# Eighty-seven gathered rows fetched by SyncE in a deformable-convolution kernel

## The chip, the cores and the metric

The kernel runs on one core of one Trainium2 chip. The metric is the device time of the whole launch in microseconds (us). The engines of the core are TensorE (PE; its weight loads are listed apart as PEld), VectorE (DVE), ScalarE (ACT), GpSimd (POOL) and SyncE (SP). SP does no arithmetic here: it issues DMAs through its own queue (SPq). POOL issues the indirect DMAs (gathers).

## The reference, cut to what matters

The input is x, 4 images of 128 channels and 128 x 128 pixels. Two layers are computed; all that matters for this change lies in the first step of layer 0, a deformable 3 x 3 convolution on the channel-normalised image:

```python
offset = conv(x, w_off)                       # 18 offsets for each pixel
py, px = base_y + dy, base_x + dx             # 9 sampling points (taps) for each pixel
sampled = sum over 4 corners of x[:, corner] * bilinear weight
out = einsum('bckhw,ock->bohw', sampled, w_conv)
```

Where a pixel samples depends on the data, so its four corners must be fetched by an index that is known only at run time. After it come a mixture of 8 experts (top 2), a Fourier-domain channel mix, which the kernel does as a flip and one matmul, and a router over 64 experts that picks 8 tokens for each; their results are added to those tokens.

## The kernel before, in words

**Tables.** For each image the kernel normalises the channels and writes a table to HBM (`table_of`, line 688, and `block`, line 530). An entry of the table is 1 KB: two image rows of one column, 128 channels each. Two neighbouring entries, 2 KB in one piece, hold the four corners of a sampling point. `positions` turns the offsets into the index of the first entry (line 677) and into four weights. The offsets themselves come from a convolution by matmuls over padded rows: `padding` (line 458) copies four transposed rows into one of four pad tiles, and `offsets` (line 467) runs six matmuls over two of them. Image 0's table is built at the start; the table of each next image is built while the present one is sampled.

**Sampling.** An image has 32 groups of four rows, a group has 9 taps, and one tap of one group is a `Chunk` (line 764): 288 an image, 1152 in all. For a chunk, `gather` (line 771) has POOL issue four indirect DMAs, one for each row, each fetching 128 positions x 2 KB into the tile `g` (128 x 4 x 4 x 128 float32). `weighted` has DVE multiply three of the rows by their weights (all four where the tap is 0); `weighted_too` has ACT do the fourth row in four instructions; `summed` has PE transpose and add the corners (16 transposing matmuls into PSUM, named trg); `moved` has ACT copy that to sT; and eight matmuls or more add it to `sums` by the convolution's weights (`convolved`, line 734). The pool of `g` has AHEAD = 6 buffers, so the gathers of chunk n + 6 are issued when PE has read chunk n.

**Order.** Every engine works through its instructions in the order in which they are written out. The main loop (line 1621) writes chunk after chunk; each chunk is two turns (`tick`). `Turns` (line 117) runs the rest as small jobs that yield for some turns: the experts, the flip, the router, the next image's table. SP's instructions stand in that same order: a DMA of SP that waits for an engine holds up every later one of SP. In the sampling SP carries the table stores (table<-ent), the loads of the image (xc, xg) and the stores of finished rows (x_d<-x).

SP's DMAs take eight completion semaphores in turn. A DMA that takes one first waits until the DMA that had it before has landed, so at most eight of SP's DMAs are under way. POOL's gathers have eight semaphores of their own.

**What else the change touches.** A tile of zeros, `blank` (line 342), is the weight of the matmul that clears `sums`. While image 3 is sampled, expert weights are loaded into places that are free by then, among them the first 512 columns of the four pads (`flat_pads`, lines 335 and 1655).

Of the kernel before, what the change touches and what calls it, by code (L numbers as in the profile page):

```python
# [42 lines left out]
F32 = mybir.dt.float32  # L43
I32 = mybir.dt.int32
U32 = mybir.dt.uint32
AF = mybir.ActivationFunctionType
ALU = mybir.AluOpType
AX = mybir.AxisListType
# [3 lines left out]
P = 128  # L52
# [5 lines left out]
HID = 512  # L58
# [6 lines left out]
TAPS = 9  # L65
EPS_C = 1e-6
EPS_T = 1e-5
RB = 8
CB = 16
TW = P + 1  # L70
TC = P + 2
# [14 lines left out]
BANKS = 6  # L86
AFTER = 11
SPACE = 13
BLOCK = 84
FILL = "fill"  # L90
DONE = "done"
# [98 lines left out]
def metaformer_kernel(  # L190
# [50 lines left out]
    with ExitStack() as main:  # L241
# [91 lines left out]
        for pad in pads:  # L333
            nc.vector.memset(pad, 0.0)
        flat_pads = [pad.rearrange("p y x -> p (y x)")[:, 0:HID].unsqueeze(1) for pad in pads]
        aT_sb = wts.tile([P, P], F32, name="aT_sb")

        gwT_sb = wts.tile([P, 2 * E1], F32, name="gwT_sb")
        gb_sb = wts.tile([P, 1], F32, name="gb_sb")


        blank = wts.tile([P, P], F32, name="blank")
        nc.vector.memset(blank, 0.0)
        flip = wts.tile([P, P], F32, name="flip")
        nc.gpsimd.memset(flip, 0.0)
        for base in (0, -P):
# [108 lines left out]
                yield from with_bias(ew_sb[:, 4 * h : 4 * h + 4, :], biases[h])  # L455


        def padding(t, h, row, read, padded):

            yield FILL  # L460
            tr = transposes(row, 4)
            read.append(h)
            yield turns.hop
            eng.scalar.copy(pads[(2 * t + h) % 4][:, :, 1 : P + 1], tr)
            padded.append(h)

        def offsets(im, t, padded):

            while len(padded) < 2:
                yield 1  # L470
            yield 1


            yield FILL
            po = bank([P, 4, P], "po")
            for k in range(3):
                for h in range(2):
                    eng.tensor.matmul(
                        po[h * P // 2 : (h + 1) * P // 2],
                        lhsT=woff_sb[:, k, :],  # L480
                        rhs=pads[(2 * t + h) % 4][:, :, k : k + P],
                        start=(k == 0),
                        stop=(k == 2),
                    )
            yield turns.hop
# [13 lines left out]
            yield turns.hop  # L499
            if i0 == 0:  # L500
                im.z[q] = pa.tile([P, CB + 2, 6 * TAPS], F32, name=f"z{im.b}_{q}", tag="z")
                if q == 0:
                    eng.vector.memset(im.z[q][:, 0, :], 0.0)
                else:
                    eng.scalar.copy(im.z[q - 1][:, CB + 1, :], tr[:, 0, 0, 0 : 6 * TAPS])
            eng.scalar.copy(
                im.z[q][:, 1 + i0 : 1 + i0 + RB, :].rearrange("p (h i) o -> p h i o", h=2),
                tr[:, :, :, 0 : 6 * TAPS].rearrange("p i h o -> p h i o"),
            )
            if i0 == 0 and q > 0:  # L510
# [192 lines left out]
        class Group:  # L703
# [30 lines left out]
            def convolved(self, k):  # L734

                yield 1
                if k + 1 < FIRST:
                    return
                if k + 1 == FIRST:
                    eng.tensor.matmul(  # L740
                        sums.rearrange("p s c -> p (s c)"),
                        lhsT=blank,
                        rhs=iota,
                        start=True,
                        stop=False,
                    )
# [13 lines left out]
                if k + 1 == TAPS:  # L760
                    yield turns.hop
                    yield from mixed(self)

        class Chunk:


            def __init__(self, group, k):
                self.group, self.k = group, k
                self.shared = k > 0

            def gather(self):
                self.g = pg.tile([P, 4, 4, P], F32, name="g", tag="g")
                im = self.group.im
                for s, y in enumerate(self.group.rows):
                    eng.gpsimd.indirect_dma_start(
                        out=self.g[:, s].rearrange("p v c -> p (v c)"),
                        out_offset=None,
                        in_=im.table,
                        in_offset=bass.IndirectOffsetOnAxis(
                            ap=im.index[:, y, self.k : self.k + 1], axis=0  # L780
                        ),
                    )

            def weighted(self):
                n = 3 if self.shared else 4
# [4 lines left out]
                )  # L790

            def weighted_too(self):
                g, y = self.g[:, 3], self.group.rows[3]
                w = self.group.im.weight[y // CB]
                for v in range(4):
                    eng.scalar.activation(
                        g[:, v, :], g[:, v, :], AF.Copy, scale=w[:, y % CB, self.k, v : v + 1]
                    )

            def summed(self):  # L800

                self.tr = bank([P, 4, P], "trg")
                for s in range(4):
                    for v in range(4):
                        eng.tensor.matmul(
                            self.tr[:, s, :],
                            lhsT=self.g[:, s, v, :],
                            rhs=ident,
                            is_transpose=True,
                            start=(v == 0),  # L810
                            stop=(v == 3),
                        )

            def moved(self):
# [2 lines left out]
                eng.scalar.copy(group.sT[self.k], self.tr)  # L817
                turns.start(group.convolved(self.k))


        exps = []

# [766 lines left out]

        def in_turn():  # L1590

            for b in range(NB):
                for number, (rows_of, minus, runs) in enumerate(orders[b]):
                    im = images[b]
                    if im.sent <= P // RB or not im.weight.keys() >= {y // CB for y in rows_of}:
                        raise ValueError("a table is late")
                    group = Group(images[b], number, rows_of, minus, runs)
                    group.begin()
                    for k in range(TAPS):
                        chunk = Chunk(group, k)  # L1600
                        chunk.gather()
                        yield chunk

        source = in_turn()
        chunk = [next(source) for _ in range(AHEAD)]
        turns.hop = HOP
# [5 lines left out]
        def tick(more):  # L1612

            turns.fills(0)
            turns.slot += 1
            if more and total - QUICK <= n <= total:
                turns.steps()
                turns.fills(0)
                turns.slot += 1

        while n < total + 3 or turns.jobs:
# [14 lines left out]
            if 0 <= n < total:  # L1636
                chunk[n].summed()
                turns.fill()
            tick(False)
            if 0 <= n - 1 < total:  # L1640
                chunk[n - 1].moved()
            turns.steps()
            if n >= 0 and n + 3 < total and (n + 3) % TAPS == 0:
                chunk[n + 3].group.weights((n + 3) // TAPS % 2)
            tick(True)
            if n == LATE * slots:
# [8 lines left out]
                rooms = [[part(), part()], [part(), part()], flat_pads]  # L1655
# [100 lines left out]
```

## Time and profile before

| | |
|---|---|
| Time, median of 3 runs | 7746.31 us (7738.57 to 7773.56) |
| The profiled execution: its own time | 7753.58 us |
| Its span, first to last instruction | 7751.8 us |
| Sampling, first gather to the last trg | 120.1 to about 7569 us |
| Mean granted TensorE clock | 0.879 |
| DMA bytes moved | 1526.15 MB, 1210.35 of them on the gathers' queue |

All times are of one execution. Busy shares are means over the whole span. A group of the page's list is named by line, engine, operation and tiles; nearly all instructions are recorded by one helper, line 104, so the tiles tell what they are. "Idle before" is time in which the engine did nothing ahead of an instruction of the group, with what ended it: "issue" means that nothing the profile shows was waited for.

### The profile page before, as it was taken

The numbers are of one execution on the slowest core, as the hardware profiler recorded it, in microseconds if no ns is written. First come the engines' busy times: TensorE is split into PE (matmuls) and PEld (weight loads), VectorE is DVE, ScalarE is ACT, GpSimd is POOL, SyncE is SP. The second block draws the span as 40 slices with busy tenths as digits, with TensorE's granted clock in tenths as the row PEclk, the third lists the DMA queues.
The fourth block names the chain that finished last, engine by engine and source line by source line (L and its number), as shares of the span: only waits on it lengthen the run. The fifth ranks groups of instructions, "written<-read, shape, count | busy, mean of one in ns | idle before, by whom it ended". The sixth has DMA issues, their size and how long they took to land.

```text
span 7751.8 us, 118020 instructions
## 1 busy us (share of the span) xinstructions
PE 6164.8 (80%) x38823; PEld 4942.0 (64%) x38823; DVE 4872.4 (63%) x15420; ACT 3844.8 (50%) x9910; POOL 4474.6 (58%) x4795
## 2 busy tenths in 40 slices
PE   5778888788878878888788788888777888888875
PEld 3666666666666666666666666666666666767663
DVE  5566666666566666666666666666667655666663
ACT  4455555554455555554455555555444444454442
POOL 5655555556555555565655555555666656655650
PEclk8888888888888889898888898888888998898987
DMA  7566665666665666665666666666655676777657
GB/s 223 177 196 184 190 193 184 193 182 180 189 191 181 188 188 189 190 192 176 188 189 189 189 188 189 190 188 183 197 179 173 221 256 184 240 266 258 186 170 266
DMA packets 579234, 1526.15 MB, mean 197 GB/s; under 512 B 86456, under 2 KB 225408, under 8 KB 578624
## 3 DMA queue, kind: packets, MB, share of 16 engines
q0 software_dynamic: 369664, 1210.35, 51.3%
q1 hardware_dynamic: 206656, 299.87, 11.5%
q8 instruction: 310, 5.08, 0.3%
q10 hardware_dynamic: 2304, 8.39, 0.3%
q14 instruction: 300, 2.46, 0.1%
HBM read 1381.43 MB, written 136.85 MB: 196 GB/s over the span
## 4 chain that ended last, share of the span: by engine, by line
PE 66%; issue 17%; DVE 7%; ACT 3%; another core or an unknown queue 3%; DMA 3%; POOL 2%; POOLq 0%; DVEq 0%; ACTq 0%; SPq 0%
PE trg L104 27%; PE sums L104 16%; PE pe L104 11%; PE tr L104 4%; PE po L104 3%; DVE g L104 2%; DMA g<-table,index 2%; DVE x L104 2%; POOL g L104 2%; PE ps L104 1%; PE small L104 1%; PE pq L104 1%; PE pf L104 1%; ACT g L104 1%
## 5 line engine op out<-in xcount | busy, mean ns | idle before, releaser
L104 POOL DMA_INDIRECT g<-table,index x4608 | 4375.0, 949 | 3030.1 <-issue 1251.6
L104 PE MATMUL trg<-ident,g 128*128 128x128 f32 x18432 | 2705.5, 300 | 774.3 <-issue 691.1
L104 PEld LDWEIGHTS trg<-ident,g 128*128 128x128 f32 x18432 | 2400.3, 157 | 1058.2 <-issue 944.1
L104 DVE TENSOR_TENSOR g<-g,small 128x1536 f32<-128x1536 f32 (+1 forms) x1152 | 2075.3, 1805 | 769.4 <-remote 349.4
L104 DVE SCALAR_TENSOR_TENSOR x<-pe,gate,x 128x128 f32<-128x128 f32 x4072 | 1394.1, 343 | 930.2 <-PE pe L104 512.8
L104 PE MATMUL sums<-wconv_sb,sT 128*128 128x128 f32 x9216 | 1389.7, 291 | 452.8 <-issue 407.5
L104 PEld LDWEIGHTS sums<-wconv_sb,sT 128*128 128x128 f32 x9216 | 1251.0, 203 | 697.9 <-issue 657.3
L104 ACT COPY sT<-trg 128x512 f32<-128x512 f32 x1152 | 667.6, 580 | 2063.3 <-remote 906.4
L104 ACT ACTIVATE g<-g,weight 128x128 f32<-128x128 f32 x4096 | 1303.4, 393 | 26.3 <-DMA g<-table,index 22.9
L104 PE MATMUL pe<-ew_sb,nT 128*128 128x512 f32 x2048 | 1119.1, 649 | 31.3 <-issue 26.7
L104 PEld LDWEIGHTS pe<-ew_sb,nT 128*128 128x128 f32 x2048 | 372.3, 213 | 221.2 <-issue 191.8
L104 DVE TENSOR_TENSOR x<-ps,x 128x512 f32<-128x512 f32 x128 | 87.9, 687 | 414.2 <-remote 254.2
L104 ACT ACT_TABLE_LOAD x263 | 337.4, 1283 | 7.5 <-DVE nmax L104 2.2
L104 ACT ACTIVATE n<-x,b_nb,b_rs 128x128 f32<-128x128 f32 x512 | 210.2, 482 | 142.6 <-DVE b_nb L104 52.2
L104 ACT ACTIVATE xn<-x,c_nb,c_rs 128x128 f32<-128x128 f32 x512 | 211.3, 485 | 137.6 <-DVE c_nb L104 72.9
L104 DVE BATCH_NORM_STATS2 b_st<-x 128x6 f32<-128x128 f32 x512 | 136.3, 283 | 191.4 <-ACT x L104 93.8
L104 ACT ACTIVATE tn<-x,d_nb,d_rs 128x128 f32<-128x128 f32 x512 | 210.9, 483 | 57.0 <-DVE d_nb L104 48.5
L104 ACT ACTIVATE c_rs<-c_mv,eps_c 128x4 f32<-128x4 f32 x128 | 38.0, 297 | 401.5 <-DVE c_mv L104 266.7
L104 PE MATMUL po<-pad,woff_sb 128*64 128x512 f32 x768 | 199.6, 633 | 4.0 <-issue 3.7
L104 PEld LDWEIGHTS sums<-ident,xg 128*128 128x128 f32 x1024 | 139.7, 196 | 84.5 <-issue 84.3
L104 PE MATMUL small<-rw_sb,nT 128*128 128x8 f32 x1024 | 140.7, 252 | 64.8 <-issue 63.2
L104 PEld LDWEIGHTS small<-rw_sb,nT 128*128 128x128 f32 x1024 | 141.2, 206 | 59.5 <-issue 57.5
(236 smaller groups left out, 5326.2 us busy)
## 6 DMA issues: line engine op xcount, KB each, us to landing
g<-table,index POOLq DMA_INDIRECT x4608
table<-ent SPq DMA_DIRECT2D x48, 1024.0 KB
xc<-in_x SPq DMA_DIRECT2D x64, 512.0 KB
w<-x_d SPq DMA_DIRECT2D x64, 512.0 KB
xg<-in_x SPq DMA_DIRECT2D x124, 256.0 KB
x_d<-x SPq DMA_DIRECT2D x124, 256.0 KB
out<-w SPq DMA_DIRECT2D x48, 512.0 KB
w<-in_weight SPq DMA_DIRECT2D x42, 512.0 KB
```

What stands on the lines that cost most here:

```text
L104: return self.tc.keep_in_program_order(issue(*args, **kwargs))
```

## The change

87 of the 4608 row gathers are taken from POOL and given to SP. A class `Lone` chooses, once every 13 chunks (RUN), a coming chunk whose tap isn't 0 and whose table is complete. For that chunk POOL gathers three rows; the fourth, the one that ACT weights, is fetched by SP:

- DVE scales the row's 128 indices to byte offsets (one instruction on 128 x 1). SP stores them to HBM and, seven turns later, loads them back as 4 x 32 integers in four partitions.
- SP loads them into registers, sixteen at a time, and after each load issues sixteen DMAs of 2 KB, one for each position, each written as two pieces of 1 KB. There are five DMAs a turn, so a row takes 26 turns, and the next row follows at once.
- The rows land in two tiles in turn. They are the pads 2 and 3, which the tables' `padding` gives up while sampling goes on: it then has two pads instead of four, and a job that finds its pad taken waits (`busy`).
- The chunk that uses the row is weighted some six to seven turns after the row's last DMA is written out.
- `blank` becomes the first 128 columns of another tile of zeros, and two of the `flat_pads` places for expert weights become two tiles of the pool of weights.

```diff
+        apart = [
+            pad.rearrange("p y x -> p (y x)")[:, 0:HID].rearrange("p (v c) -> p v c", c=P)
+            for pad in pads[2:]
+        ]
+        busy = [False, False]
+        places = [wts.tile([4, P // 4], I32, name=f"places{i}") for i in range(2)]
+        scaled = [wts.tile([P, 1], I32, name=f"scaled{i}") for i in range(2)]
...
+        def pad_of(t, h):
+            return pads[(2 * t + h) % 4 if turns.hop == 1 else h]
...
+            while turns.hop > 1 and busy[h]:
+                yield 1
+            busy[h] = True
...
                 for s, y in enumerate(self.group.rows):
+                    if s == 3 and self.lone is not None:
+                        continue
                     eng.gpsimd.indirect_dma_start(
...
+            def look(self, t):
+
+                i, begin = len(self.users), max(t + 16, self.end)
+                n = (begin + 2 * RUN + 7) // 2 + 1
+                n += n % TAPS == 0
...
+            def job(self, i, n, im, index, begin):
+                row = self.found[i]
+                eng.vector.tensor_scalar(scaled[i % 2], index, 8.0 * P, None, ALU.mult)
+                yield
+                yield
+                eng.sync.dma_start(out=row.unsqueeze(1), in_=scaled[i % 2])
+                for _ in range(7):
+                    yield
+                eng.sync.dma_start(out=places[i % 2], in_=row.rearrange("(a c) -> a c", a=4))
+                while self.now < begin:
+                    yield
...
+                for p in range(P):
+                    if p % 16 == 0:
+                        a, c = divmod(p, P // 4)
+                        loads, values = nc.values_load_multi_w_load_instructions(
+                            places[i % 2][a : a + 1, c : c + 16],
+                            engines=[mybir.EngineType.SP],
...
+                    eng.sync.dma_start(
+                        out=apart[i % 2][p : p + 1]
+                        .rearrange("p (h v) c -> p h (v c)", h=2)
+                        .bitcast(U8),
+                        in_=flat[bass.ds(values[p % 16], 16 * P)]
+                        .rearrange("(o h c) -> o h c", o=1, h=2),
+                    )
+                    if p % (P // (2 * RUN) + 1) == P // (2 * RUN):
+                        yield
...
+            def turn(self, t):
+                self.now = t
+                if self.filling is not None and next(self.filling, DONE) is DONE:
+                    self.filling = None
+                if self.ahead is None:
+                    self.look(t)
+                if self.ahead is not None:
+                    next(self.ahead)
...
+                lone.turn(2 * n)
             tick(False)
...
+                lone.turn(2 * n + 1)
```

More of the change, by code (lines that the diff above doesn't have):

```diff
@@ L45 @@
 U32 = mybir.dt.uint32
+U8 = mybir.dt.uint8
 AF = mybir.ActivationFunctionType
@@ L88 @@
 SPACE = 13
+RUN = 13
 BLOCK = 84
@@ L339, in metaformer_kernel @@
         gb_sb = wts.tile([P, 1], F32, name="gb_sb")
-        blank = wts.tile([P, P], F32, name="blank")
-        nc.vector.memset(blank, 0.0)
         flip = wts.tile([P, P], F32, name="flip")
@@ L463, in padding @@
             yield turns.hop
-            eng.scalar.copy(pads[(2 * t + h) % 4][:, :, 1 : P + 1], tr)
+            eng.scalar.copy(pad_of(t, h)[:, :, 1 : P + 1], tr)
             padded.append(h)
@@ L480, in offsets @@
                         lhsT=woff_sb[:, k, :],
-                        rhs=pads[(2 * t + h) % 4][:, :, k : k + P],
+                        rhs=pad_of(t, h)[:, :, k : k + P],
                         start=(k == 0),
@@ L484, in offsets @@
                     )
+            busy[:] = [False, False]
             yield turns.hop
@@ L741, in convolved @@
                         sums.rearrange("p s c -> p (s c)"),
-                        lhsT=blank,
+                        lhsT=zeros[:, 0:P],
                         rhs=iota,
@@ L769, in __init__ @@
                 self.shared = k > 0
+                self.lone = None
             def gather(self):
@@ L782, in gather, with last @@
                     )
+            def last(self):
+                return self.g[:, 3] if self.lone is None else self.lone
             def weighted(self):
@@ L792, in weighted_too @@
             def weighted_too(self):
-                g, y = self.g[:, 3], self.group.rows[3]
+                g, y = self.last(), self.group.rows[3]
                 w = self.group.im.weight[y // CB]
@@ L803, in summed @@
                 for s in range(4):
+                    g = self.g[:, s] if s < 3 else self.last()
                     for v in range(4):
@@ L806, in summed @@
                             self.tr[:, s, :],
-                            lhsT=self.g[:, s, v, :],
+                            lhsT=g[:, v, :],
                             rhs=ident,
@@ L818, in moved, with __init__ @@
                 turns.start(group.convolved(self.k))
+        class Lone:
+            def __init__(self):
+                self.found = dram.tile([total // RUN + 2, P], I32, name="found")
+                self.tiles, self.users, self.end = {}, [], 0
+                self.ahead = self.filling = None
+                self.values = []
+            def look(self, t):
+                i, begin = len(self.users), max(t + 16, self.end)
+                n = (begin + 2 * RUN + 7) // 2 + 1
+                n += n % TAPS == 0
+                b, k = divmod(n, slots)
+                number, k = divmod(k, TAPS)
+                if n >= total or b not in images or i > 1 and begin <= 2 * self.users[-2]:
+                    return
+                im, y = images[b], orders[b][number][0][3]
+                if im.sent <= P // RB or im.known <= y // CB:
+                    return
+                self.users.append(n)
+                self.tiles[n] = apart[i % 2]
+                self.end = begin + 2 * RUN
+                self.ahead = self.job(i, n, im, im.index[:, y, k : k + 1], begin)
+            def job(self, i, n, im, index, begin):
[9 more added lines that the diff above has]
+                    yield
+                self.filling, self.ahead = self.ahead, None
+                flat = im.table.rearrange("e c -> (e c)").bitcast(U8)
+                values = []
+                for p in range(P):
[4 more added lines that the diff above has]
+                            engines=[mybir.EngineType.SP],
+                            min_val=0,
+                            max_val=8 * P * (TW * TC - 2),
+                            skip_runtime_bounds_check_because="positions are clamped to the table",
+                        )
+                        for load in loads:
+                            tc.keep_in_program_order(load)
+                    eng.sync.dma_start(
[4 more added lines that the diff above has]
+                        .rearrange("(o h c) -> o h c", o=1, h=2),
+                    )
+                    if p % (P // (2 * RUN) + 1) == P // (2 * RUN):
+                        yield
+                if self.now >= 2 * n - 2:
+                    raise ValueError("a row is late")
+            def turn(self, t):
[6 more added lines that the diff above has]
+                    next(self.ahead)
@@ L1590, in in_turn @@
         def in_turn():
+            n = 0
             for b in range(NB):
@@ L1600, in in_turn @@
                         chunk = Chunk(group, k)
+                        chunk.lone = lone.tiles.get(n)
+                        n += 1
                         chunk.gather()
                         yield chunk
+        lone = Lone()
         source = in_turn()
@@ L1642, in metaformer_kernel @@
             turns.steps()
+            if 0 <= n < total:
+                lone.turn(2 * n + 1)
             if n >= 0 and n + 3 < total and (n + 3) % TAPS == 0:
@@ L1653, in metaformer_kernel @@
                 part = lambda: late.tile([P, 2, HID], F32, name="w", tag="w", bufs=4)
-                rooms = [[part(), part()], [part(), part()], flat_pads]
+                spare = lambda: pw.tile(
+                    [P, 1, HID], F32, name="w", tag="weight", bufs=3 * P // CB // 2
+                )
+                rooms = [[part(), part()], [part(), part()], flat_pads[0:2]]
+                rooms[-1] += [spare(), spare()]
                 rooms.append([pw.tile([P, 2, HID], F32, name="w", tag="index")])
```

## The prediction, as put on record

> **What bounds the kernel now.** I read the page's busy shares first, then the chain of work that ended last, then PE's and POOL's waits, and last the rows of the operations that the change moves.
>
> ```profile
> PE 6164.8 (80%) x38823; PEld 4942.0 (64%) x38823; DVE 4872.4 (63%) x15420; ACT 3844.8 (50%) x9910; POOL 4474.6 (58%) x4795
> ...
> PE 66%; issue 17%; DVE 7%; ACT 3%; another core or an unknown queue 3%; DMA 3%; POOL 2%; POOLq 0%; DVEq 0%; ACTq 0%; SPq 0%
> ...
> L104 POOL DMA_INDIRECT g<-table,index x4608 | 4375.0, 949 | 3030.1 <-issue 1251.6
> L104 PE MATMUL trg<-ident,g 128*128 128x128 f32 x18432 | 2705.5, 300 | 774.3 <-issue 691.1
> ```
>
> In the chain the reader is to see that PE's own work and PE standing still for no recorded reason ("issue") make 83%, POOL and the DMAs 5%. A gather costs POOL 949 ns and a gap of 306 ns (the median gap between two), 1.255 us; four make 5.02 us. A chunk lasts (7569 - 120) / 1152 = 6.47 us. So POOL isn't the bound: it runs ahead and stops for a free buffer. The list of waits says the same:
>
> ```profile
> POOL g L104 <- issue: 1251.6, 3669, 8.6
> POOL g L104 <- ACT sT L104: 1097.1, 344, 9.1
> ...
> PE trg L104 <- issue: 691.1, 814, 4.7
> PE sums L104 <- issue: 424.6, 532, 2.6
> ...
> PE trg L104 <- DMA g<-table,index: 14.3, 17, 1.7
> ```
>
> POOL's gaps over 0.45 us, counted in the trace, are 683, nearly all before a chunk's first gather, and never are more than 12 gathers (three chunks) issued without one. PE's waits for a gather's landing are some 20 us in all. What PE loses it loses by "issue", 1322 us over its rows. The timeline of PE shows how that looks:
>
> ```profile
> 3015.78 0.60 PE L104 MATMUL trg<-ident,g 128*128 128x128 f32 x4
> 3016.79 0.27 PE L104 MATMUL trg<-ident,g 128*128 128x128 f32 x1 [0.41 <-issue]
> 3018.21 0.27 PE L104 MATMUL trg<-ident,g 128*128 128x128 f32 x1 [1.15 <-issue]
> 3018.96 0.31 PE L104 MATMUL trg<-ident,g 128*128 128x128 f32 x1 [0.48 <-issue]
> 3021.06 0.27 PE L104 MATMUL trg<-ident,g 128*128 128x128 f32 x1 [1.79 <-issue]
> ```
>
> The inputs of these transposes were ready, and yet one goes every 0.7 or 1.4 us; DVE, ACT and then POOL run dry behind it. The trace doesn't name the cause. Two things speak for the gather traffic having a part: pauses over 0.4 us are 34 in 1000 PE instructions in the sampling, but 2 to 4 in 1000 in the first 120 us and the last 110 us, which have no gathers (PE is less dense there, too); and in bins of 2 us the pause grows from 0.15 us in the quarter of bins with the least gather traffic to 0.53 us in that with the most, while SP's traffic makes no difference (0.35 and 0.34). That is an association, not a proof.
>
> **The change part by part.**
>
> *87 gathers leave POOL.* The bounds: nothing, if all of them were hidden, and 87 x 1.255 = 109 us, if POOL's time were the kernel's. I value a gather by what goes with the gather traffic. PE's pauses: 1322 / 4608 = 0.287 us a gather. The slower clock after pauses, read as mean less median duration: trg 18432 x (300 - 273) ns = 498 us, sums 9216 x (291 - 275) = 147, pe 2048 x (649 - 593) = 115; 760 us in all, 0.165 a gather. The chain's stretches on gathers, DMA 1.9% and POOL 1.7%, 279 us, 0.061 a gather. Sum 0.513 us; 87 of them are **45 us**. This is a choice: it puts all of PE's pauses down to gathers, in proportion. It is nearer to the lower end, as POOL's slack demands.
>
> *The fourth row comes through SP.* 87 x 128 = 11,136 DMAs of 2 KB, 696 register loads, 174 DMAs for indices. If SP keeps up and the rows land in time, this lies beside PE and costs nothing. SP has 13 x 6.47 = 84 us for a row. What one such DMA costs SP shows only roughly:
>
> ```profile
> L104 SPq DMA_DIRECT2D table<-ent x51: 332/367/373, 482.7 to 5407.9; - x51
> ...
> L104 SPq DMA_DIRECT2D table<-zeros x8: 462/616/1180, 2.8 to 3822.1; - x8
> ```
>
> Nearest in shape are four of the eight border stores (one partition's worth, two pieces of 1 KB): 583 to 624 ns in the sampling, each right behind another DMA. A store issued alone takes 367 ns. The second bound is the eight semaphores: two border stores of 2 KB landed 3.8 and 4.7 us after their issue, and eight under way give one in 0.48 to 0.59 us. I take 0.5 us: 64 us a row. A register load isn't in the trace; the bounds are 0.02 us (SP's shortest semaphore instruction) and 2 us (SP's fastest landings); I take 0.5 us, eight make 4 us. SP's other work in the sampling, 553 DMAs, took 249 us, 2.8 us in 84. Sum **71 of 84 us**; with 0.61 us a DMA 85, and with the dearest loads 97. So SP has little to spare, and the ends lie on both sides of its budget.
>
> *Waits on SP.* SP now stops for finished rows (SPq <- DVE x, 2583 us in 81 waits) with nothing due. After the change the next group's xg and the lone DMAs queue behind such a wait. They are written out in the turn in which DVE gets there, so SP is late by little, and a row has six to seven turns (21 us) less a landing of 4 us in hand; xg is written out six chunks (39 us) ahead. Cost nothing; without that cover, see the first rival.
>
> *DMA traffic.* A gather leaves 80 packets (369,664 / 4640 DMAs on that queue); a lone row leaves two data packets and two or more completions for each of 128 DMAs, some 512. That is 87 x 432 = 37,600 more of 579,234, 6.5%. The bytes stay the same; the DMA share (0.62) hardly moves. The trace has 46 ns as the median packet of SP's queue. Bounds: nothing, and the third rival.
>
> By the Trainium skill's page "DMA: Bandwidth & Descriptors", section "Why a DMA increments its semaphore by 16 and not by 1", a DMA is spread over the largest number up to 16 that divides its slowest dimension, on the lowest-numbered engines: two pieces mean that all 11,136 DMAs go through two of the sixteen engines. No row here lists a packet's engine; taking the rule with 11,136 packets of 46 ns, those two would be busier by 0.5 ms, an estimate of 0.62 + 0.07, which costs no time by itself but makes their queues longer.
>
> *DVE, ACT, the rest.* 87 scalings on DVE (160 ns for a 128x4 instruction) are 14 us on an engine busy 63%: beside PE. ACT's weighting of the row is as before, with a wait for up to eight semaphores more; ACT is busy 50%. Two pads instead of four: a new table's block is due every 30 turns, a repeated one of image 0 every 13, and pad and offsets are done in about ten, so at most a job shifts by a turn. `blank` and the moved expert weights cost nothing: the same instructions on other tiles, and the places are free by then. Bounds of these: 0 to 14 us; I take 0.
>
> *Sum.* The profiled execution took 7753.58 us: 7753.58 - 45 = 7709. It stood 7.3 us above the median of 7746.31, so the forecast is 7746.31 - 45 = **7702 us** (-0.58%).
>
> **Rivals.**
>
> 1. *SP becomes the bound* (slower). Place: SP's queue. At 0.61 us a DMA and 1 us a load a row takes 78 + 8 + 2.8 = 89 us, 5 us over its 84. The 17 us in hand are gone after three or four rows; then ACT waits for the row, PE for ACT, and each of some 83 rows adds 5 us: 415 us, **about 8115 us**. It decides from (84 - 2.8 - 4) / 128 = 0.60 us a DMA. For it: the 583 to 624 ns of the border stores and the landings of 4 us. Against it: those stores stood behind larger DMAs, and a lone store takes 367 ns.
> 2. *The gathers were hidden anyway* (no change). The pauses have another cause, and POOL only waits longer: **7746 us**, 7725 to 7765. For it: 683 waits of POOL for buffers and hardly any of PE for gathers.
> 3. *The small packets disturb PE* (slower). If pauses and the slower clock (2082 us) go with the number of packets, 6.5% more is 135 us, up to 7881; with half of that **about 7810 us**. For it: the pauses' tie to DMA traffic. Against: SP's traffic, much of it in 1 KB packets, shows no tie.
> 4. *The change doesn't do what it says*: fewer rows than 87 find a place, or few are taken in time; then it is rival 2.
>
> **How the numbers follow.** The forecast's mechanism with its range of 7640 to 7730 gets 0.50, about 0.37 of it beyond 0.5%; no change (rivals 2 and 4) 0.20; SP as the bound 0.17; packets 0.13, a little of it within 0.5%. Half a per cent, 39 us, is about what measurement of this kernel can tell from no change. So faster 0.37, same 0.34, slower 0.29. The range runs from the forecast's lower end (109 us off) to the packets' upper end, 7640 to 7880, and leaves out SP as the bound. The likeliest case alone: 7640 to 7730.
>
> **What would show it.** Right: 4521 gathers; SP's DMAs at 0.4 to 0.55 us; ACT's wait before g as short as now (26 us in all); PE's "issue" some 25 us shorter; mean clock a little above 0.879. Rival 1: ACT waits for the pads' tiles, SP issues without a gap. Rival 2: POOL's waits longer by some 109 us and PE's rows unchanged. Rival 3: PE's "issue" longer at the same waits. I am wrong altogether if PE's pauses come from its own instruction stream, or if a small DMA of SP costs over 0.6 us.

## The result, and the profile after

The changed kernel takes 8424.32 us (median of 6 runs, 8413.57 to 8460.80), the kernel before beside it 7742.60 us: 1.0885 times as long, 95% interval 1.0855 to 1.0915. The forecast was 7702 us, with a range up to 7880. The time went the way of the first rival (8115 us) and beyond it.

The page of the changed kernel, the lines that answer to those of before (its chain of waits breaks off after 4% of the span and says nothing):

```profile
PE 6104.7 (73%) x38823; PEld 4943.4 (59%) x38823; DVE 4864.2 (58%) x15506; ACT 3818.8 (45%) x9910; POOL 4380.8 (52%) x4708
...
L106 POOL DMA_INDIRECT g<-table,index x4521 | 4282.2, 947 | 3785.5 <-issue 1469.6
L106 PE MATMUL trg<-ident,g 128*128 128x128 f32 x18084 | 2535.1, 296 | 496.5 <-issue 369.4
...
L106 PE MATMUL sums<-wconv_sb,sT 128*128 128x128 f32 x9216 | 1404.9, 298 | 959.1 <-ACT sT L106 563.0
...
L106 ACT ACTIVATE pad<-pad,weight 128x128 f32<-128x128 f32 x348 | 111.0, 390 | 1211.7 <-DMA pad<-table 1170.0
```

87 gathers are gone (4521), PE is busy as long as before, but 73% of a longer span. New is the last line: 348 ACT instructions on 87 rows, with 1170 us of waiting for the row ahead of them. The list of waits, longest first:

```profile
POOL g L106 <- issue: 1469.6, 3610, 15.7
ACT pad L106 <- DMA pad<-table: 1170.0, 67, 26.7
POOL g L106 <- ACT sT L106: 1042.2, 345, 31.8
...
PE trg L106 <- issue: 384.2, 390, 14.8
```

67 of the 87 rows came late, by up to 27 us. PE's pauses without a reason became fewer (384 us on trg, 691 before; 1022 in all, 1322 before), while PE now also stands still behind ACT's late sT (563 us on sums); the mean granted clock fell from 0.879 to 0.846. What SP did, first by instruction (shortest, median and longest in ns), then in its timeline:

```profile
L106 SPq MOVE pad<-table x11136: 1/29/2351, 150.2 to 8183.3; - x199
L106 SPq DMA_DIRECT2D pad<-table x11136: 1/228/3832, 150.3 to 8183.4; - x199
```

```profile
3019.80 7.86 SPq L106 DMA_DIRECT2D pad<-table  x20
3027.76 0.37 SPq L106 DMA_DIRECT2D found<-scaled  x1
3028.22 27.25 SPq L106 DMA_DIRECT2D pad<-table  x35
3055.50 0.70 SPq L106 DMA_DIRECT2D places<-found  x1
```

A position takes two instructions, a register move (29 ns) and the DMA (228 ns), 0.325 us from one position to the next when nothing disturbs. But SP never rests, and its pace changes: 20 positions in 7.9 us, then, behind the store of the indices (found<-scaled), 35 in 27.3 us.

The instructions' starts on SP, summed by kind over the first three images, give a row's cost: 77.1 us for 128 positions (0.60 each), 9.3 us for eight register loads (1.16 each), 4.4 us for SP's other work, together **90.8 us**. A row has 13 chunks, which lasted 84.1 us before. Of the 660 us that the profiled execution grew by (8411.7 against 7751.8 us), 394 came in the first three images (their last chunk ended at 6102 us, before at 5708), about what 66 rows x 6 to 7 us give, and 266 in the last image.

### The profile page after: what moved, and what is told of

It reads as the page before. It is cut to its first block, busy times and chain, and to the rows that moved or that the text cites. A ratio compares the mean times of both kernels' runs of the same rounds, so it can differ in the third digit from the quotient of the medians.

```text
span 8411.7 us, 141272 instructions
## 1 busy us (share of the span) xinstructions
PE 6104.7 (73%) x38823; PEld 4943.4 (59%) x38823; DVE 4864.2 (58%) x15506; ACT 3818.8 (45%) x9910; POOL 4380.8 (52%) x4708
## 5 line engine op out<-in xcount | busy, mean ns | idle before, releaser
L106 POOL DMA_INDIRECT g<-table,index x4521 | 4282.2, 947 | 3785.5 <-issue 1469.6
L106 PE MATMUL trg<-ident,g 128*128 128x128 f32 x18084 | 2535.1, 296 | 496.5 <-issue 369.4
L106 PEld LDWEIGHTS trg<-ident,g 128*128 128x128 f32 x18084 | 2322.4, 155 | 679.3 <-issue 528.3
L106 PEld LDWEIGHTS sums<-wconv_sb,sT 128*128 128x128 f32 x9216 | 1279.4, 210 | 1212.6 <-ACT sT L106 595.4
L106 ACT ACTIVATE g<-g,weight 128x128 f32<-128x128 f32 x3748 | 1193.2, 393 | 31.6 <-DMA g<-table,index 19.2
L106 ACT ACTIVATE pad<-pad,weight 128x128 f32<-128x128 f32 x348 | 111.0, 390 | 1211.7 <-DMA pad<-table 1170.0
L106 PE MATMUL ps<-aT_sb,xfT 128*128 128x128 f32 x1024 | 171.7, 310 | 73.1 <-issue 61.2
L106 PEld LDWEIGHTS ps<-aT_sb,xfT 128*128 128x128 f32 x1024 | 153.5, 221 | 103.8 <-issue 83.9
L106 DVE TENSOR_SCALAR share<-e 128x4 f32<-128x4 f32 x128 | 24.1, 188 | 326.5 <-ACT e L106 275.6
```

What stands on the lines that cost most here:

```text
L106: return self.tc.keep_in_program_order(issue(*args, **kwargs))
```

## The experiments

The theory after the first look: SP's queue sets the pace, and lateness is the loss. Its rivals: the lone DMAs' packets disturb the gathers and PE, or the gathers were worth nothing. Some kernels ran on chips where the kernel before takes 6118 us instead of 7600 to 7770. PE's pauses are hardly seen there: 46 us by "issue" in the trace of half1024, which stands for the kernel before, against 1322 us. Ratios are to the kernel before on the same chip, and the time of the kernel before says which sort it was.

### Lateness: fewer rows, and a cheaper row

`RUN = 16` and `RUN = 26` instead of 13: 71 and 43 rows, with more chunks in which to fetch each.

> One row every 16 chunks in place of 13 (about 70 rows). SP's queue as the bound: a row took SP 91.7 us in the changed kernel, and 16 chunks at the pace of before are 16 x 6.47 = 103 us, so SP keeps up, ACT's wait for the pads' tiles (1170 us) falls below 100 us, and the time is 7700 to 7760 us. Shared disturbance (each small DMA of SP costs the other engines something, late or not): 70/87 of the loss of 682 us remains, about 8290 us.

> One row every 26 chunks (about 43 rows). SP's queue as the bound: SP has 168 us for 91.7 us of work; 7710 to 7760 us, ACT's wait for the pads' tiles near 0. Shared disturbance: 43/87 of 682 us remains, about 8080 us.

Measured (before: 7620.58): 7715.65 us, ratio 1.0107 (1.0069 to 1.0146), and 7669.81 us, 1.0054 (1.0034 to 1.0074). ACT's wait for the row is gone from the list of waits in the first. So lateness is seven to eight of the nine per cent (6.7 of 7.9 between after2 and run16b below, on one chip); the rest stays.

With known positions, no register work (the rows fetched are not those that the offsets ask for):

```diff
-                    if p % 16 == 0:
-                        ... register loads
-                        in_=flat[bass.ds(values[p % 16], 16 * P)]
+                        in_=flat[(p + 64 * P) * 8 * P : (p + 64 * P) * 8 * P + 16 * P]
```

> 87 rows as in the changed kernel, with all 11136 DMAs, but from fixed positions of the table: no register loads and no register moves (the 87 rows hold other table entries than the reference's). SP's queue as the bound: without loads (9.4 us a row) and moves (33.9 us a row) a row costs SP about 92 - 43 = 49 us, well under 84; 7700 to 7760 us. Shared disturbance by the DMAs and their packets: the same DMAs, so about 8400 us.

Measured: 7656.94 us, 1.0042 (1.0023 to 1.0062), 87 rows at 13 chunks. SP's positions take 63.5 us a row. Without loads and moves the row fits, with the same 11,136 DMAs, so SP's own instructions are what made it late.

### What a gather is worth

Three gathers in all 1024 chunks of a later tap, no lone rows (the fourth row is left out, ACT weights a standing tile instead):

> POOL gathers three rows in place of four in all 1024 chunks whose tap isn't 0, SP fetches nothing, ACT weights a tile that stays as it is (the fourth row is left out). It measures what a gather is worth. By the forecast's 0.513 us a gather: 7742 - 525 = about 7217 us. If the gathers are hidden behind PE: 7742 us, with POOL's waits longer by some 1024 x 1.255 = 1285 us. If POOL's time were the kernel's: 7742 - 1285 = 6457 us. PE's idle time by issue falls from 1322 us by 22% to about 1030 us if the pauses go with gathers in proportion, and stays if not.

Measured (before: 7620.58): 6261.82 us, 0.8225 (0.8185 to 0.8266): 1353 us by the ratio, through 1024: **1.32 us a gather**. PE's waits by "issue" fell from some 1300 to 462 us; the line that showed 691.1 us before now reads

```profile
PE trg L106 <- issue: 261.4, 301, 30.7
```

So the pauses do go with the gathers, and more than in proportion.

The 87 rows alone neither gathered nor fetched, on both sorts of chip:

> The other half of the change alone: the 87 rows are not gathered by POOL and not fetched by SP (their chunks weight a tile that stays as it is; the rows are left out). If a gather is worth what it was in the run without 1024 of them (1353 us / 1024 = 1.32 us at the clock of that chip), 115 us faster, ratio 0.985. By the forecast's 0.513 us: 45 us faster, 0.994. If 87 are too few to matter: 1.000.

Measured (before: 6118.28): 6018.13 us, 0.9839 (0.9822 to 0.9855), 1.15 us a gather.

> The 87 rows are neither gathered nor fetched, the upper bound of what the change can gain. Where the kernel before pauses, 87 x 1.15 to 1.32 us = 100 to 115 us less, ratio 0.985; by the prediction's 0.513 us a gather, 45 us, ratio 0.994.

Measured (before: 7610.13): 7530.86 us, 0.9903 (0.9879 to 0.9926), 0.65 to 1.06 us a gather. This is all that the change could have gained: 1 to 1.6%.

Gathers with half the bytes in 1024 chunks (half of that row is left out):

> As the run with 1024 rows left out, but POOL still issues those 1024 gathers with half the bytes each (1 KB a position; ACT weights the other half from a tile that stays as it is). If PE's pauses go with the bytes that are gathered: half the gain, ratio 0.91. If they go with POOL's instructions or with the number of descriptors: about 1.00. If each contributes, between.

Measured (before: 6118.28): 6116.14 us, 0.9996 (0.9986 to 1.0005). On this chip the bytes don't set the time; the gathers follow each other every 1.25 us (median; 1.26 on average) from the first to the last, 5804 us, so POOL's instruction does. As the time is the same, its trace can stand for the kernel before there.

The changed kernel with three gathers in all other later-tap chunks as well (their fourth row is left out), to see SP under a faster pace:

> The changed kernel as it is (one row every 13 chunks through SP), with POOL gathering three rows in all chunks of a later tap; the fourth row of the chunks that SP doesn't serve is left out and a tile that stays as it is stands in. If SP's slow steps (52 of 265 a row, 48 us of 91.7) are the same pauses as PE's and go with the gathers' traffic, a row costs SP 55 to 70 us, about what 13 chunks of 5.2 us allow, and the time is 6300 to 6600 us. If a row costs SP 92 us by itself, SP sets the pace: 1152 / 13 x 92 = 8150 us and more.

Measured (before: 6118.28): 6624.53 us, 1.0834 (1.0816 to 1.0852). Its ACT still waits for rows:

```profile
ACT pad L106 <- DMA pad<-table: 776.1, 65, 21.9
```

A row takes 55.7 + 11.0 + 3.2 = 70 us of SP in the first three images, and 13 chunks last 69. SP is the bound here, too, though this chip shows few of the pauses: a row isn't late by them alone. Where PE and SP pause it is longer by some 21 us (90.8 against 70).

### What a row costs that comes in time

The changed kernel and the one with 71 rows again, beside a kernel that cuts a position into four pieces:

> The changed kernel again, beside three others on one chip. Theory (SP's queue paces the kernel, and the pauses of about 0.7 us that its instructions share with PE's make a row last 92 us instead of 84): ratio 1.07 to 1.10 and a row of 88 to 95 us where the kernel before pauses (its time above 7500 us); where it doesn't pause (about 6118 us), a row lasts some 67 to 72 us and fits 13 chunks, which then last 13 x 5.2 = 67 us, so SP is still about at its limit: ratio 1.04 to 1.09. Rival (the row costs the same without pauses, by its DMAs alone): the ratio is 1.08 or more in both cases.

Measured (before: 7610.13): 8221.37 us, 1.0788 (1.0747 to 1.0829).

> One row in 16 chunks, 71 rows, as before, here as the partner of the kernel with four pieces: ratio 1.005 to 1.015 where the kernel before pauses; 1.02 to 1.05 where it doesn't, since two kernels with lone rows lost there. The gathers' landings reach 9 us or more at the 95th percentile.

Measured: 7702.84 us, 1.0122 (1.0095 to 1.0149).

```diff
-            pad.rearrange("p y x -> p (y x)")[:, 0:HID].rearrange("p (v c) -> p v c", c=P)
+            pad[:, :, 0:P]
...
-                        .rearrange("p (h v) c -> p h (v c)", h=2)
-                        .rearrange("(o h c) -> o h c", o=1, h=2),
+                        .rearrange("(o h c) -> o h c", o=1, h=4),
```

> As the kernel with one row in 16 chunks, but each position is written as four pieces of 512 bytes at places that don't join (the rows of the pad with their border between them), so that a DMA is four descriptors instead of one of 2 KB. Theory A (all lone DMAs go through one DMA engine, whose queue delays the gathers' share on it): the gathers' 95th percentile falls from 9 to about 7 us and the time by 0.5 to 2% against the partner, which takes it to the kernel before or below. Theory B (the loss comes with the number of DMAs and their completions): the same as the partner within 0.3%, or slower by up to 1% for the 27,000 packets more.

Measured: 9413.70 us, 1.2368 (1.2340 to 1.2396). Both theories missed. The tile view of SP says why:

```profile
L106 SPq MOVE pad<-table x9088: 2/29/2772, 149.5 to 9245.0; - x198
L106 SPq DMA_DIRECT2D pad<-table x9088: 2/577/5336, 149.5 to 9245.0; - x198
```

A DMA of four pieces takes SP 577 ns, one of a single 2 KB piece 228. A row lasts 128 us where 16 chunks lasted 103, and the kernel runs at SP's pace again. The gathers' tail did not move: the 95th percentile from issue to landing, worked out from the trace, is 8.5 us, 8.3 in its partner, 6.3 without rows (norow87b). That speaks against a crowded engine, but at a slower pace, so it doesn't settle it.

Next SP's work was added without a saving: all 4608 gathers stay, and 71 rows more are fetched and read by nobody (`chunk.lone = None`). It ran on two chips.

> The change's first half alone, at one row every 16 chunks (where SP keeps up): SP fetches its 71 rows, but POOL gathers all four rows of every chunk and nobody reads SP's. If SP's DMAs cost as much as the gathers save plus the net loss of that spacing (1.07%): 71 x 1.32 + 82 = 175 us slower, ratio 1.023. If the loss at that spacing comes from chunks waiting for their row: 1.000.

Measured (before: 6118.28): 6400.82 us, 1.0460 (1.0443 to 1.0478), 282 us by 71, 4.0 us a row, more than either expectation.

> POOL gathers all 4608 rows as in the kernel before, and SP fetches 71 rows more that nobody reads: SP's work alone, with no saving, and nobody waits for a row. On another chip a row cost 4 us so. If a lone row that is in time costs 2 us here as well (157 us over what the missing gathers give, by 71), the ratio is 1.02, and with 4 us 1.037. If SP's work costs nothing by itself (the forecast), 1.000 within 0.003.

Measured (before: 6117.75, as for the next three): 6399.87 us, 1.0464 (1.0447 to 1.0481). The next three take parts of it away: the register work, as above; the bytes; all position DMAs (`...` stands for the DMA as it was):

```diff
+                    eng.sync.dma_start(
+                        out=apart[i % 2][p : p + 1, 0, 0:16].bitcast(U8),
+                        in_=flat[bass.ds(values[p % 16], P // 2)].rearrange("(o c) -> o c", o=1),
+                    )
```

```diff
-                    eng.sync.dma_start(out=apart[i % 2][p : p + 1] ...
```

> The same with positions known beforehand: 128 DMAs of 2 KB a row, no register loads, no register moves, and addresses that follow each other. If the DMAs are what costs, the same ratio as the partner with all the work, within 0.004; if the moves and loads are, 1.005 or less.

Measured: 6376.94 us, 1.0423 (1.0406 to 1.0441).

> The same with all instructions of SP, but each DMA moves 64 bytes of its 2048. If the 2 KB packets on the DMA engines are what disturbs the gathers, the ratio falls to 1.005 or less and the gathers' landings at the 95th percentile fall by 1 us or more; if the number of DMAs, their descriptors and completions are, it stays as with 2 KB, within 0.004.

Measured: 6390.85 us, 1.0438 (1.0421 to 1.0456). Neither the bytes nor the register work cost much.

> The same without the position's DMAs: 8 register loads a row, the two DMAs for the indices and DVE's scaling are left. If the DMAs or the moves cost, 1.000 within 0.004; if the loads or the scaling do, 1.01 or more.

Measured: 6264.34 us, 1.0231 (1.0214 to 1.0248). Neither expectation applies, since this trace has no register load: with nobody using the values, they fell away. So the kernel is the one before with DVE's scaling, the two DMAs for the indices, and two pads less, and still loses 147 us, 2.1 us a row. Two pads less can't be it: the kernel without rows has them, too. What happens is seen around one store of the indices, issued at 2557.48 us. Windows of this trace, the last columns the granted clock, the DMA engines' busy share and GB/s:

```profile
core 0: us, PE busy (x) PEld busy (x) DVE busy (x) ACT busy (x) POOL busy (x), PEclk, DMA share, GB/s
2549.00:2557.00 8.00, 7.57 (x41) 6.01 (x42) 7.92 (x38) 4.03 (x9) 6.17 (x7) 0.79 0.79 243
2557.00:2559.00 2.00, 2.00 (x18) 1.87 (x17) 2.00 (x5) 1.81 (x6) 1.39 (x3) 1.00 0.76 211
2559.00:2567.00 8.00, 8.00 (x53) 6.17 (x52) 3.53 (x19) 5.24 (x15) 6.17 (x7) 1.00 0.97 69
2567.00:2575.00 8.00, 4.98 (x31) 4.74 (x29) 7.16 (x20) 5.03 (x15) 5.36 (x7) 0.79 0.89 334
```

For 8 us after the store's 128 elements of 4 bytes the engines are 97% busy and move 69 GB/s instead of 243. Single packets of the gathers take up to 7 us there. DVE, which weights what has landed, falls to 3.5 of 8 us, and afterwards PE to 5.0. Over the whole trace, gathers issued 0 to 4 us behind such a store land after 10.5 to 10.9 us (medians), those issued 4 to 20 us ahead of one after 3.7. It is the same in the traces of the changed kernel (10.3 and 9.8 against 3.6), run16, run26 and fixed: all have that store. POOL's waits for landings show it, in this kernel and in the one with no rows:

```profile
POOL g L106 <- DMA g<-table,index: 239.1, 430, 4.9
```

```profile
POOL g L106 <- DMA g<-table,index: 125.2, 411, 0.3
```

### The store of the indices

In the changed kernel at 13 chunks a row, PE and DVE move the indices instead of the two DMAs:

```diff
-                eng.sync.dma_start(out=row.unsqueeze(1), in_=scaled[i % 2])
...
-                eng.sync.dma_start(out=places[i % 2], in_=row.rearrange("(a c) -> a c", a=4))
...
+                    moved = bank([P, P], "moved")[0:1, :]
+                    eng.tensor.transpose(moved, scaled[i % 2], ident)
+                    yield turns.hop
+                    eng.vector.tensor_copy(places[i % 2], moved)
```

> The changed kernel at 13 chunks a row, with only the staging of the indices changed: instead of a store of 128 elements of 4 bytes to HBM and a load back, PE transposes the scaled column (one transpose of 128x1) and DVE copies it to one partition as integers; no DMA. Theory (in seven traces, four of which take no gather away, the gathers issued around the store land after 10 us instead of 3.6, since the store of 4-byte elements stops the DMA queues for some 7 us, and SP issues 2 to 3 lone DMAs in the first 8 us behind it where 11 are due in undisturbed stretches): a row loses about 5 us, from 92 to 86 to 87 us where the kernel before pauses (its time above 7500 us), ratio 0.985 to 1.03 instead of 1.08 to 1.09, and the gathers' landings at the 95th percentile fall from 9 to about 6 us. Where it doesn't pause (6118 us), a row is about 63 us in 67, ratio 0.98 to 1.02. Rival (the store's stall is absorbed, and SP's row is long by the pauses alone): ratio 1.06 or more where the kernel before pauses, a row of 90 us or more.

Measured (before: 6118.37): 6204.00 us, 1.0142 (1.0125 to 1.0159). In the first three images only 0.1% of the gathers land after more than 8 us (12 to 13% with the store and 16 chunks a row, on these chips), and POOL's line is

```profile
POOL g L106 <- DMA g<-table,index: 68.0, 223, 0.3
```

The ratio lies in the range expected for a chip without pauses. But the theory and its rival were set apart for chips with pauses, and the changed kernel itself was not run on one without. So by how much the transpose shortens a late row where PE and SP pause isn't shown.

At 16 chunks a row, with the store kept but 512 bytes for each index:

```diff
-                eng.vector.tensor_scalar(scaled[i % 2], index, 8.0 * P, None, ALU.mult)
-                eng.sync.dma_start(out=row.unsqueeze(1), in_=scaled[i % 2])
+                eng.vector.tensor_scalar(scaled[i % 2], index.to_broadcast([P, P]), 8.0 * P, None, ALU.mult)
+                eng.sync.dma_start(out=row, in_=scaled[i % 2])
...
+                eng.sync.dma_start(out=places[i % 2].unsqueeze(2),
+                    in_=row.rearrange("(a c) w -> a c w", a=4)[:, :, 0:1])
```

> One row in 16 chunks, the indices staged over HBM as in the change, by the same two DMAs, but each index is written as 512 bytes (128 copies of it) instead of 4, and the load back picks one integer of each. If elements of 4 bytes written to HBM are what stops the queues, no gather lands late behind the store, and the kernel gains some 2 us a row on its partner's 1.011: 0.985 to 1.000 where the kernel before pauses. If any store of 128 pieces does it, or the load back does, late landings stay and the ratio is 1.007 to 1.015.

Measured (before: 6118.37): 6178.92 us, 1.0101 (1.0084 to 1.0118); in the first three images fewer than 0.5% of the gathers land after more than 8 us. Those issued 0 to 4 us behind the store land after 4.1 to 4.2 us. The time alone would also fit the rival, whose range was 1.007 to 1.015; the landings decide, and beside sponly16b the time agrees: it is 221 us less, of which 71 gathers at 1.15 us are 82, and the other 139 us are 2.0 us a row (an estimate). So the same two DMAs with 512 bytes an index stop nothing, and 4-byte elements do. The 128 small elements also lie side by side in 512 bytes of HBM, while the wide ones lie apart: whether it is their size or their place was not separated.

Both are still slower than before, and the place is seen when the end of chunk 864, the last of the third image, is read from the traces on the chips without pauses (us; the kernel before took 6118 on all of them):

| kernel | chunk 864 ends | from there to the end of chunk 1152 |
|---|---|---|
| half1024 (stands for before) | 4467 | 1467 |
| norow87 | 4388 | 1442 |
| pe13 | 4388 | 1634 |
| wide16 | 4397 | 1596 |
| sploads16 | 4572 | 1508 |
| sponly16b | 4555 | 1655 |

Through three images the kernel with the transpose is level with the one that fetches no row at all: its 66 rows cost nothing, and the gathers' 79 us are gained. In the last image it loses 192 us to norow87, 9 us for each of some 21 rows. The same two kernels by windows of the first three images and of the last, first norow87, then pe13:

```profile
150.00:4360.00 4210.00, 3868.99 (x27407) 3172.34 (x27408) 3482.63 (x11193) 2793.34 (x7317) 3186.36 (x3360) 0.98 0.79 242
4400.00:5800.00 1400.00, 1279.89 (x9581) 1068.91 (x9581) 1153.82 (x3388) 854.87 (x2208) 1058.72 (x1117) 0.97 0.84 275
```

```profile
150.00:4360.00 4210.00, 3890.87 (x27473) 3182.82 (x27472) 3498.54 (x11330) 2798.71 (x7315) 3185.63 (x3361) 0.98 0.80 245
4400.00:5800.00 1400.00, 1173.52 (x8385) 972.35 (x8386) 995.89 (x2958) 740.43 (x1906) 913.58 (x964) 0.92 0.78 249
```

POOL issues 3361 and 3360 instructions in the first window, 964 and 1117 in the second. There SP also carries the expert weights, the outputs and the tokens, 173 large DMAs in pe13's trace: a row takes 74 us of SP instead of 64, and the waits with nothing due that SP had are gone (447 us for DVE's x in norow87, 10 in pe13). The table fits SP's order as what holds the last image up: only the kernels with position DMAs lose much there. ACT's waits from 4400 to 6000 us show one place, again norow87, then pe13:

```profile
ACT w L106 <- DMA out<-w: 40.7, 12, 6.3
```

```profile
ACT w L106 <- DMA out<-w: 143.9, 26, 12.2
```

A buffer of w comes free when its output has been stored, and 48 of the 64 stores stand in SP's queue among the lone DMAs. In wide16 the wait is 105.4 us, although SP has 16 chunks for a row and no row is late; in sploads16, which has no position DMAs, it is 25.2 (from 4560 to 6200 us). That this order costs the whole loss wasn't tried by itself.

## Why the prediction was wrong, point by point

- **SP's row, 71 of 84 us: the step that failed.** It is 90.8 us. The position was put at 0.50 us and took 0.60, just the point from which the first rival decides; a register load was put at 0.5 us and took 1.16. The quiet cost is lower than forecast (0.325 us a position), but two things that the sum lacked come on top. SP's instructions suffer pauses of 0.7 and 1.4 us as PE's do, on moves, too, which wait for nothing: some 52 steps of a row are over 0.45 us and take 48 us together, against 8 steps and 13 us on a chip without pauses (after_norow). They are the same pauses at least in part: in the first three images 68% of PE's pauses over 0.4 us end within 0.06 us of the end of such a step of SP, and 6% do when SP's times are shifted by 20 us. And the store of the indices holds up the lone DMAs behind it: SP's positions take 55.7 us a row with it (after_norow) and 49.9 without it (pe13), 6 us, and 58.8 (sponly16b) against 51.2 with the wide store (wide16), 8 us; both pairs differ in their gathers, too. What the pauses are stays open; they go with the number of gathers (norow1024), and are nearly absent on some chips.
- **Rival 1 had mechanism, place and signs right.** It gave 89 us a row, 5 us over, 415 us. Measured are 6.7 us over, 394 us in three images, and 266 more in the last one, where a row takes 97 us; the rival took all images as alike, as did I.
- **"Waits on SP cost nothing", "DVE, ACT, the rest: 0 to 14 us".** The scaling itself is nothing: pe13 has it and is level with norow87 through three images. The store and the load behind it are named as 174 DMAs, but neither the sum of SP's row nor that of the packets has them. The store costs 2 us a row in time (sploads16), by the landing of the gathers. No bound in the prediction reached it.
- **DMA traffic at nothing, rival 3.** Wrong as put: it isn't the number of packets. 9088 lone DMAs add two packets each (one of data, one of completion) and cost nothing in the first three images on the chips without pauses (sponly16b ends chunk 864 no later than sploads16); 71 stores of 4-byte elements, 9088 small packets, cost 147 us. The prediction took from the Trainium skill's page "DMA: Bandwidth & Descriptors", section "Why a DMA increments its semaphore by 16 and not by 1", that two pieces go through two engines. The trace has the DMA as one element of 2048 bytes: the two pieces join, and by the page's rule that would be one engine. Its queue is not what delays the gathers, since sptiny16 with 64 bytes a DMA has the same time and pe13 with the full DMAs has no late gathers. The same page's section "Why small descriptors are slow (HBM only)" counts small pieces' overhead in cycles a packet and in bytes of descriptors; a stop of 8 us for other queues' packets is beyond what it states.
- **A gather's worth, 0.513 us: too small.** It is 0.65 to 1.06 us for 87 gathers on a chip with pauses, 1.15 without, 1.32 when 1024 go. I took PE's pauses in proportion to the gathers, and with 1024 gone they fall faster; without pauses POOL's 1.25 us is simply the bound. This error was on the safe side and decided nothing.
- **The hidden gathers (rival 2)** fell with norow87, and rival 4 with 87 rows and 11,136 DMAs in the trace.

Why the change loses, then: at RUN = 13 lateness (7 to 8 of 9%); beyond it 2 us a row for the store, against 1 us saved; and up to 9 us a row in the last image. The last two prices are from chips without pauses. With pauses both places are seen as well: run16b ends chunk 864 at 5608 us, norow87b on the same chip at 5500, which is 1.8 us for each of 54 rows when the 12 gathers more are taken off (an estimate), and from there it loses 76 us more. No kernel here with lone rows beats the one before. The traces point to one that was not tried: the transpose in place of the store, and lone rows in the first three images only. By the table it would be 79 us ahead at chunk 864 where there are no pauses, 6118 - 79 = 6039 us, an estimate; where PE and SP pause, a row without the store would by the same kind of estimate still take some 85 us (90.8 - 6) of the 84, so RUN would have to be larger.

## What to carry to other kernels

An engine that only issues DMAs is a bound like any other: add up every instruction of its queue per period, registers and waits too, allow for the pauses that the other engines show, and do it for each stretch of the program, since the budget of one image isn't that of the next. Small staging transfers deserve as much care as the bulk: look for elements of a few bytes written to HBM, and move such a column with a transpose on the chip or widen its elements. And where a change loses, compare the times at which the same chunk ends in two traces: it showed in one table what the totals had hidden.

## What the runs showed of the hardware

- Behind a store of 128 elements of 4 bytes to 512 bytes of HBM, single packets of the gathers take up to 7 us (69 GB/s at 97% busy engines); behind one with 512 bytes an element, gathers land as fast as elsewhere (4.1 us).
- Issuing a DMA from SP took 228 ns with one piece of 2 KB and 577 ns with four pieces of 512 bytes (medians). A load of 16 registers took 1.2 us.
- Pauses of about 0.7 and 1.4 us come on SP and PE, on register moves too, and 68% of PE's end together with one of SP's. On some chips they were nearly absent (46 us of PE's time instead of 1322), and the same kernel took 6118 instead of 7600 us.
